# A four-layer vision kernel: spectral pieces that ride beside the scans, and the order inside a scan step

## The chip, the cores and the metric

One core of one Trainium2 chip runs the whole kernel. The metric is the device time of one execution in microseconds (us). The kernel before takes 27,082.73 us (median of three runs, 27,078.75 to 27,084.66). All arithmetic is in fp32.

## The reference, cut to what matters

Eight images of 64 x 64 pixels with 96 channels go through four residual layers, each on a group-normalised input:

```python
x = x + L0(gn(x))   # selective scan: 192 channels x 16 states, four scan directions
x = x + L1(gn(x))   # chunked scan
x = x + L2(gn(x))   # selective scan again, other weights
x = x + L3(gn(x))   # spectral: upsample x2, W1, quadratic, W2, low pass, every second pixel

def step(h, inp):                     # inside L0 and L2
    dA = exp(dt[..., None] * A)
    h = h * dA + (dt * u)[..., None] * b
    y = einsum('bkdn,bkn->bkd', h, c)
```

The four directions k = 0 to 3 are: along the rows, along the columns, along the rows backwards, along the columns backwards. For k = 1 and 3 the reference transposes the image ("wh"), so position 0, 1, 2, ... of the scan are pixels 64 floats apart in the kernel's row-major tiles.

In L3 the Fourier transforms are fixed 64 x 128 and 128 x 64 matrices, so that the layer is a chain of matmuls: up along one axis, up along the other, a hidden layer of 384 with a square, a mix back to 96, down along one axis, down along the other, and the residual.

## The kernel before, in words

The eight images are worked one after the other. For each one the program runs L0, L1 and L2 and the work between them. L3 of an image is not run there: it is cut into small pieces which are slipped into the two selective scans of the *next* image. So the two scans of image 0 have no pieces, the other 14 have; the L3 of the last image runs alone at the end (`spectral_layer`).

**A selective scan** (`selective_scan`) has 32 steps: four directions k times eight chunks c of 512 positions. A step has six units n = 0 to 5. One unit holds 32 channels x 16 states, as 128 partitions x 4 groups of 512 positions. The global unit is t = 6 i + n in step i. The order is written out by hand (`manual_schedule`); every engine works its own queue strictly in that order. Per unit:

- ACT: `decays(t, p)` (L855), two exps for each of two PSUM tiles `da0` and `da1`; `leave` (L886) copies the last column of h to `state`; `enter` (L826) puts the start state of a later unit in place.
- DVE: `scan(t, p)` (L870), two scans of 1026; `with_b` (L840) makes `db` = du x b, on DVE for four units of six and on POOL for n = 2 and 5.
- POOL: `h = h * c` (L891), after `state` has been copied out of h. Five `h` buffers.
- PE: `spread(t)` (L834) copies du to all partitions in PSUM (`pu`, tag "misc").

Per step, `total_y(i, hf)` sums over the states on PE (L898 adds the earlier y, L908 twelve matmuls) into `py`; the sum for units 0 to 2 is issued in unit 3, that for units 3 to 5 in unit 0 of the next step. ACT copies `py` to `y`: at L993 in unit 4, and at L1007 in unit 1. Both are `nc.scalar.copy(*sums)`. Before the change the one in unit 4 stands **ahead** of the exps of that unit, the one in unit 1 behind the first pair of them.

`prepare(i)` is a generator that makes a step's inputs two steps ahead, one part at each `prepare_part` call: matmul `pv` (L742), copy to `raw` (L747), matmul `pv` (L751), copy (L755), then the transfers `bcd` and `b`, two softplus (L775) with the change of activation table before and after them, `dd`, the transfers `dx` and `c`, `du` on POOL (L793 for wh steps, L799 for row steps), `dud`, `du2`, and the second `dx`.

PSUM has eight banks: `da0` and `da1` take three each, `py` one, `misc` one. The `py` bank is shared, in this order, by `total_y`, the `pv` of `prepare`, and most of the pieces; each waits until the one before it has been copied out by ACT.

**The pieces** (`slow_layer`, run by `Beside`). A piece is some matmuls into one PSUM bank (`begin`) and one ACT operation that empties it (`end`); some have a transfer as load before them or as store behind. First scan of an image: 16 x (T, A) (`rows`: transpose, up), two empty places, then 15 columns groups `cols`; second scan: 17 `cols`, two empty places, 16 x E (`ends`). One `cols` before is seven pieces: D, h, h, h, m, m, L (down_h; three hidden; two halves of the mix, each 8 matmuls and a copy of 192; lower). So the two scans have 139 and 137 pieces, and a step takes four or five. The places of a step are:

1. begin in unit 1 after the first exps, end at the end of unit 1 (bank py)
2. begin at the start of unit 2, end in the middle of it (py)
3. begin in the middle of unit 2, end at its end (py)
4. begin at the start of unit 4, end in the middle of it (misc)
5. begin at the start of unit 5, end right after (misc), only in steps with five pieces

All transfers of the pieces are issued by SP (`nc.sync.dma_start`): L451, L484, L495, L569, L581, L583, L614. Loads are issued up to four pieces ahead (`ends`: one), stores when the next piece begins (`flush`).

For wh steps, `view` reads u or y with the position running along the column, that is 64 floats apart, and `cut` gives the 512 positions of a chunk as 8 columns x 64 rows.

Of the kernel before, what the change touches and what calls it, by code (L numbers as in the profile page):

```python
# [17 lines left out]
DM = 96  # L18
# [4 lines left out]
LC = 512  # L23
# [44 lines left out]
def tile_vision_stack(  # L68
# [19 lines left out]
    nc = tc.nc  # L88
# [337 lines left out]

    def cut(t, wh):

        return t.rearrange("p (w h) -> p w h", h=64) if wh else t
# [3 lines left out]
    def slow_layer(prev):  # L433
# [12 lines left out]
        def rows(j):  # L446

            def load():
                if j % 2 == 0:
                    live["xs", j] = xs = wide("sx")[:DM]  # L450
                    nc.sync.dma_start(xs, xd[:, j * 256 : j * 256 + 512])  # L451
# [31 lines left out]
            def store():  # L483
                nc.sync.dma_start(  # L484
# [6 lines left out]
        def cols(n):  # L491

            def load():
                live["c1"] = c1 = narrow("sc", "x1")[:64]
                nc.sync.dma_start(c1, x1d[:, 4 * n : 4 * n + 4])  # L495
# [30 lines left out]
            for p in range(2):  # L526

                def mix(ps, p=p):
                    for i in range(2):
                        at = (2 * p + i) * 128  # L530
                        po = ps[:, i * DM : i * DM + DM]
                        nc.tensor.matmul(
                            po, live["x2"][:, at : at + 128], w12, start=True, stop=False
                        )
                        for m in range(3):
                            nc.tensor.matmul(
                                po,
                                live["f"][m][:, at : at + 128],
                                w2q[:, m, :],
                                start=False,  # L540
                                stop=(m == 2),
                            )

                def mixed(ps, p=p):
                    if p == 0:
                        live["g"] = narrow("sg", "g")
                    nc.scalar.copy(
                        live["g"][:, 2 * p : 2 * p + 2, :].rearrange("p i c -> p (i c)"),
                        ps[:, : 2 * DM],
                    )  # L550

                ops.append((None, None, mix, mixed, None, 0))
# [15 lines left out]
            def store():  # L568
                nc.sync.dma_start(  # L569
# [6 lines left out]
        def ends(j):  # L576

            def load():
                if j % 2 == 0:
                    live["xr", j // 2] = xr = wide("sr")[:DM]  # L580
                    nc.sync.dma_start(xr, xd[:, j * 256 : j * 256 + 512])  # L581
                live["g2", j] = g2 = narrow("s3", "g" if j % 2 else "x1")
                nc.sync.dma_start(g2, g2d[:, 4 * j : 4 * j + 4])  # L583
# [29 lines left out]
            def store():  # L613
                nc.sync.dma_start(  # L614
# [14 lines left out]
    class Beside:  # L629

        def __init__(self, ops):
            self.ops, self.at, self.waiting, self.loaded = ops, 0, None, 0
# [22 lines left out]
        def flush(self):  # L655
            if self.waiting:
                self.waiting()
                self.waiting = None

        def begin(self, pool, tag):  # L660
# [3 lines left out]
            if op:  # L664
                ps = pool.tile([128, LC], F32, name="ps", tag=tag)
                op[2](ps)
                self.flush()
                self.open = (op, ps)
            else:
                self.flush()  # L670
                self.open = (None, None)

        def end(self):
# [4 lines left out]
            if op:  # L678
                op[3](ps)
                self.waiting = op[4]  # L680
            self.at += 1
            if self.loaded <= self.at < len(self.ops):
                self.flush()
                while self.loaded <= self.at:
                    self.load(self.loaded)
# [4 lines left out]
    def selective_scan(w, wdt, a, d, u, y, beside):  # L690
# [23 lines left out]
        with (  # L714
# [14 lines left out]
            def prepare(i):  # L729
# [3 lines left out]
                uv = [view(u[:, hf, :], wh, at, LC) for hf in range(2)]  # L733
# [13 lines left out]
                nc.scalar.copy(raw[:DM, 1, :], pv[:DM])  # L747
# [7 lines left out]
                nc.scalar.copy(raw[:, 0, :], pv)  # L755
# [137 lines left out]
            def total_y(i, hf):  # L893
# [7 lines left out]
                    view((u if k == 0 else y)[:, hf, :], wh, c * LC, LC),  # L901
# [4 lines left out]
                for g in range(NSG):  # L906
                    for q in range(3):
                        nc.tensor.matmul(  # L908
                            py[32 * q : 32 * q + 32, :],
                            red,  # L910
                            hs[q][:, g, :],
# [3 lines left out]
                return view(y[:, hf, :], wh, c * LC, LC), cut(py, wh)  # L915
# [17 lines left out]
            with tc.tile_pool(name="p_conv", bufs=2, space=PSUM) as pvp:  # L933
# [13 lines left out]
                for _ in range(5):  # L947
# [6 lines left out]
                for _ in range(2):  # L954
# [8 lines left out]
            with tc.tile_pool(name="p_da", bufs=1, space=PSUM) as pap:  # L963
# [12 lines left out]
                for t in range(total + 2):  # L976
# [5 lines left out]
                    elif n == 5 and quota > 4:  # L982
# [789 lines left out]
```

## Time and profile before

| | us |
|---|---|
| median of the runs | 27,082.73 |
| the profiled execution's own time | 27,082.74 |
| its span | 27,080.9 |
| 16 selective scans, first to last DVE scan, together | 19,215 |
| one scan without pieces (image 0) | 1,195.2 and 1,194.9 |
| scans with pieces, first of an image | 1,197 to 1,204 |
| scans with pieces, second of an image | 1,203 to 1,207 |
| a step: first DVE scan to the first of the next, without pieces, from the fifth on | 37.57 mean |
| the shortest steps | 36.25 |

A step's length is read from the timeline of DVE: twelve scans (L870) make a step, and the start of the first one is its beginning. The table's scans are the stretches from the first of 384 scans to the end of the last. The lines of the timeline merge instructions that follow each other; the bracket at the end is the idle time before them and what ended it.

### The profile page before, as it was taken

The numbers are of one execution on the slowest core, as the hardware profiler recorded it, in microseconds if no ns is written. First come the engines' busy times: TensorE is split into PE (matmuls) and PEld (weight loads), VectorE is DVE, ScalarE is ACT, GpSimd is POOL, SyncE is SP. The second block draws the span as 40 slices with busy tenths as digits, with TensorE's granted clock in tenths as the row PEclk, the third lists the DMA queues.
The fourth block names the chain that finished last, engine by engine and source line by source line (L and its number), as shares of the span: only waits on it lengthen the run. The fifth ranks groups of instructions, "written<-read, shape, count | busy, mean of one in ns | idle before, by whom it ended". The sixth has DMA issues, their size and how long they took to land. (4 is left out here: it accounts for less than half of the span.)

```text
span 27080.9 us, 283056 instructions
## 1 busy us (share of the span) xinstructions
PE 22624.0 (84%) x91061; PEld 8150.5 (30%) x91061; DVE 23966.2 (88%) x17105; ACT 16539.7 (61%) x29953; POOL 21781.7 (80%) x8360
## 2 busy tenths in 40 slices
PE   7787788888888888888888888888888888888888
PEld 2141122422224222242222422224222342223424
DVE  8989899798997989979898898988989889898896
ACT  5656566466665656556565565655656556565564
POOL 8949898498984979859797697976979769797694
PEclk7687777877778777787777877778777787778878
DMA  4415454154541545415453254532545325453252
GB/s 121 119 30 124 114 130 117 31 131 122 132 111 35 133 117 137 103 44 132 116 136 98 50 132 118 135 92 56 133 119 134 85 62 133 118 134 78 70 133 67
DMA packets 1681704, 2831.72 MB, mean 105 GB/s; under 512 B 434984, under 2 KB 478280, under 8 KB 1675616
## 3 DMA queue, kind: packets, MB, share of 16 engines
q1 hardware_dynamic: 1663584, 2807.32, 41.9%
q8 instruction: 730, 11.96, 0.2%
q10 hardware_dynamic: 16640, 6.29, 0.1%
q14 instruction: 750, 6.14, 0.1%
HBM read 2385.11 MB, written 427.49 MB: 104 GB/s over the span
## 5 line engine op out<-in xcount | busy, mean ns | idle before, releaser
L870 DVE TENSOR_TENSOR_SCAN h<-da,db 128x1026 f32<-128x1026 f32 x6144 | 13765.8, 2282 | 900.6 <-ACT da L855 479.2
L891 POOL TENSOR_TENSOR h<-h,c 128x2048 f32<-128x2048 f32 x3072 | 12769.4, 4174 | 726.0 <-ACT state L886 510.1
L908 PE MATMUL py<-h,cst 128*32 128x512 f32 x24576 | 5301.4, 795 | 69.9 <-POOL h L891 69.8
L855 ACT ACTIVATE da<-dx,a2s 128x512 f32<-128x512 f32 x6144 | 4236.4, 690 | 1508.7 <-DVE h L870 1366.6
L855 ACT ACTIVATE da<-dx,a0s 128x512 f32<-128x512 f32 x6144 | 4235.8, 690 | 1481.8 <-DVE h L870 1344.3
L840 POOL TENSOR_TENSOR db<-du,b 128x2048 f32<-128x2048 f32 x1024 | 4648.2, 4539 | 567.6 <-ACT db L826 567.6
L840 DVE TENSOR_TENSOR db<-pu,b 128x2048 f32<-128x2048 f32 x2048 | 4643.9, 2268 | 110.9 <-PE pu L834 100.6
L834 PE MATMUL pu<-du,cst 32*128 32x512 f32 x4096 | 3239.2, 881 | 1007.4 <-DVE db L840 799.9
L908 PEld LDWEIGHTS py<-h,cst 128*32 128x32 f32 x24576 | 1175.0, 142 | 4827.3 <-issue 4517.4
L751 PE MATMUL pv<-u,wk 96*128 96x512 f32 x2048 | 1816.9, 1030 | 688.4 <-ACT raw L747 685.8
L898 PE MATMUL py<-y,cst 96*96 96x512 f32 x1536 | 1517.0, 1084 | 397.9 <-ACT raw L755 395.4
L834 PEld LDWEIGHTS pu<-du,cst 32*128 32x128 f32 x4096 | 790.4, 239 | 3079.7 <-issue 1361.9
L742 PE MATMUL pv<-u,wk 96*96 96x512 f32 x2048 | 1452.4, 838 | 186.7 <-ACT y L993 142.6
L1285 ACT ACTIVATE sg<-sg 128x768 f32<-128x768 f32 x1024 | 819.6, 800 | 859.1 <-PE sg L1269 859.1
L993 ACT COPY y<-py 96x512 f32<-96x512 f32 x512 | 417.5, 815 | 1411.4 <-PE py L908 1411.4
L516 PE MATMUL ps<-s,w3as 96*128 96x512 f32 x1344 | 912.4, 767 | 327.7 <-ACT sf L523 188.1
L1239 POOL TENSOR_TENSOR ce<-ec,cr 112x512 f32<-112x512 f32 x256 | 530.8, 2074 | 719.1 <-ACT ec L1237 700.8
L1317 DVE TENSOR_TENSOR wt<-wt,cbm 128x768 f32<-128x768 f32 x1024 | 985.3, 997 | 136.6 <-ACT wt L1286 136.1
L886 ACT COPY state<-h 128x4 f32<-128x4 f32 x3072 | 597.5, 194 | 782.5 <-DVE h L870 776.8
L751 PEld LDWEIGHTS pv<-u,wk 96*128 96x128 f32 x2048 | 540.6, 291 | 1740.2 <-ACT raw L747 1212.5
L319 POOL TENSOR_SCALAR xn<-xs,sb 96x512 f32<-96x512 f32 x192 | 198.1, 1033 | 991.7 <-PE pz L324 495.6
L1216 POOL TENSOR_TENSOR rr<-lr,cc 128x768 f32<-128x768 f32 x256 | 376.6, 1471 | 754.1 <-ACT lr L1214 749.2
(241 smaller groups left out, 30790.9 us busy)
## 6 DMA issues: line engine op xcount, KB each, us to landing
dx<-dd SPq DMA_DIRECT2D x4096, 192.0 KB
b<-bcd SPq DMA_DIRECT2D x2048, 256.0 KB
c<-bcd SPq DMA_DIRECT2D x2048, 256.0 KB
du<-dud SPq DMA_DIRECT2D x2048, 128.0 KB
dd<-raw SPq DMA_DIRECT2D x1024, 192.0 KB
dud<-du SPq DMA_DIRECT2D x512, 128.0 KB
xd<-xs SPq DMA_DIRECT2D x256, 192.0 KB
cr<-bcd SPq DMA_DIRECT2D x1536, 32.0 KB
```

The costliest lines, as they stand in the source:

```text
L516: nc.tensor.matmul(ps, w3as[:, m * 128 : (m + 1) * 128], live["x2"], start=True, stop=True)
L742: nc.tensor.matmul(pv[:DM], weights[k][:, hi, 128:], uv[hi], start=(hi == 0), stop=(hi == 1))
L751: nc.tensor.matmul(pv, weights[k][:, hi, :128], uv[hi], start=(hi == 0), stop=(hi == 1))
L834: nc.tensor.matmul(pu, sel[rows, :], m["du"][rows, n // 3, :], start=True, stop=True)
L840: (nc.gpsimd if pool else nc.vector).tensor_mul(groups(m["db", n]), (m["du2"][:, n // 3, :] if pool else m["pu"]) .unsqueeze(1) .to_broadc ...
L855: nc.scalar.activation(dst[:, g, :LC], made[i]["dx"][n // 3][:, n % 3, :], AF.Exp, scale=av4[:, k, n, gs : gs + 1],)
L870: nc.vector.tensor_tensor_scan(made[i]["h", n][:, at][:, way], das[p][:, rev : 2 * SEG + rev][:, way], made[i]["db", n][:, at][:, way], 0. ...
L891: nc.gpsimd.tensor_mul(h, h, made[i]["c"])
L898: nc.tensor.matmul(py, skip[:, hf, :] if k == 0 else ident[:DM, :DM], view((u if k == 0 else y)[:, hf, :], wh, c * LC, LC), start=True, st ...
L908: nc.tensor.matmul(py[32 * q : 32 * q + 32, :], red, hs[q][:, g, :], start=False, stop=(g == NSG - 1),)
L1285: nc.scalar.activation(sg, sg, AF.Abs)
L1317: nc.vector.tensor_mul(it["wt"], it["wt"], m["cbm"][:, j : j + 1, :].to_broadcast([128, RK, Q]),)
```

## The change

Four things, three in the scan step and one in the pieces.

1. **Pieces.** All seven transfers are issued by ACT (`nc.scalar.dma_start`). The two halves m, m become one piece of 16 matmuls and one copy of 384. A store is issued right behind its copy; `flush` is gone. There is no fifth place: the scans now have 124 and 120 pieces, three or four in a step.
2. **y's copy in unit 4** (was L993) moves behind the first pair of exps of that unit.
3. **prepare in eight parts** in place of seven: the copy to `raw` at L747 is cut from the matmul at L751 by a new `yield`. Both copies to `raw` now stand at the end of a unit (4 and 5), behind all exps of it; the `pv` matmuls stand at the start of units 4 and 5. The second copy, `bcd` and `b` come in unit 5 rather than in unit 0 of the next step. The `spread` for unit 0 of the next step moves from the start of unit 5 to unit 4, ahead of the first `pv`.
4. **Columns.** For wh steps PE reads u and y with `near`: for each of the 64 rows, 8 neighbouring floats. The results in PSUM are then in the order (row, column). `turn_back` reads them in column order for the copies to `raw` (ACT reads PSUM 8 floats apart, writes one after the other), and the L908 matmuls of wh steps write PSUM 8 floats apart. y's copies of wh steps read PSUM straight and write runs of 8, where before they wrote single floats 64 apart.

```diff
+    def near(t, wh, at, n):
+        if not wh:
+            return t[:, at : at + n]
+        return t.rearrange("p (h w) -> p h w", w=64)[:, :, at // 64 : (at + n) // 64]
+    def turn_back(t, wh, n):
+        return t.rearrange("p (h w) -> p w h", w=n // 64) if wh else t
...
-                nc.sync.dma_start(c1, x1d[:, 4 * n : 4 * n + 4])
+                nc.scalar.dma_start(c1, x1d[:, 4 * n : 4 * n + 4])
...
-            for p in range(2):
-                def mix(ps, p=p):
-                    for i in range(2):
+            def mix(ps):
+                for i in range(4):
...
+            def mixed(ps):
+                live["g"] = narrow("sg", "g")
+                nc.scalar.copy(live["g"].rearrange("p i c -> p (i c)"), ps[:, : 4 * DM])
...
             if op:
                 op[3](ps)
-                self.waiting = op[4]
+                if op[4]:
+                    op[4]()
             self.at += 1
-            if self.loaded <= self.at < len(self.ops):
-                self.flush()
-                while self.loaded <= self.at:
-                    self.load(self.loaded)
+            while self.loaded <= self.at < len(self.ops):
+                self.load(self.loaded)
...
-                uv = [view(u[:, hf, :], wh, at, LC) for hf in range(2)]
+                uv = [near(u[:, hf, :], wh, at, LC) for hf in range(2)]
...
-                nc.scalar.copy(raw[:DM, 1, :], pv[:DM])
+                nc.scalar.copy(cut(raw[:DM, 1, :], wh), turn_back(pv[:DM], wh, LC))
+                yield
...
-                nc.scalar.copy(raw[:, 0, :], pv)
+                nc.scalar.copy(cut(raw[:, 0, :], wh), turn_back(pv, wh, LC))
...
-                    view((u if k == 0 else y)[:, hf, :], wh, c * LC, LC),
+                    near((u if k == 0 else y)[:, hf, :], wh, c * LC, LC),
...
-                            py[32 * q : 32 * q + 32, :],
+                            turn_back(py[32 * q : 32 * q + 32, :], wh, LC),
                             red,
-                            hs[q][:, g, :],
+                            cut(hs[q][:, g, :], wh),
...
-                return view(y[:, hf, :], wh, c * LC, LC), cut(py, wh)
+                py = py.rearrange("p (h w) -> p h w", h=64) if wh else py
+                return near(y[:, hf, :], wh, c * LC, LC), py
...
                     if n == 2 and quota > 1:
                         other.begin(pyp, "py")
-                    elif n == 5 and quota > 4:
-                        other.begin(pmp, "misc")
-                    if n in (0, 3, 5) and ahead:
+                    if n in (0, 3) and ahead:
                         spread(t + 1)
...
                     elif n == 4:
-                        nc.scalar.copy(*sums)
                         if quota > 3:
                             other.begin(pmp, "misc")
+                        if t + 2 < total:
+                            spread(t + 2)
                         prepare_part(i + 2)
-                    if n == 5:
-                        other.end()
+                    elif n == 5:
+                        prepare_part(i + 2)
                     if t < total:
                         scan(t, 0)
...
                     elif n == 4:
+                        nc.scalar.copy(*sums)
                         other.end()
-                    elif n == 0:
-                        prepare_part(i + 1)
-                    elif n == 5:
-                        prepare_part(i + 2)
...
                     if n in (1, 2):
                         other.end()
+                    if n in (4, 5):
+                        prepare_part(i + 2)
                     if n in (0, 1, 5):
                         prepare_part(i + 1)
```

The calls ahead of the loop follow: six parts of `prepare(0)` where there were five, and four parts of `prepare(1)` where there were two.

## The prediction

> **What bounds the kernel now.** I read the page first, for the busy shares, then the groups, then who waits for whom, and last the timeline of one step engine by engine. The page's first part:
>
> ```profile
> PE 22624.0 (84%) x91061; PEld 8150.5 (30%) x91061; DVE 23966.2 (88%) x17105; ACT 16539.7 (61%) x29953; POOL 21781.7 (80%) x8360
> ```
>
> No engine is full. The costliest groups say where the time lies:
>
> ```profile
> L870 DVE TENSOR_TENSOR_SCAN h<-da,db 128x1026 f32<-128x1026 f32 x6144 | 13765.8, 2282 | 900.6 <-ACT da L855 479.2
> L891 POOL TENSOR_TENSOR h<-h,c 128x2048 f32<-128x2048 f32 x3072 | 12769.4, 4174 | 726.0 <-ACT state L886 510.1
> L993 ACT COPY y<-py 96x512 f32<-96x512 f32 x512 | 417.5, 815 | 1411.4 <-PE py L908 1411.4
> ```
>
> The 16 selective scans take 19,215 of the span's 27,080.9 us, and all edits are in them; the other 7,866 us I leave as they are. Inside a scan DVE and POOL do nearly the same amount: in a plain step of 37.55 us (timeline below) POOL idles only 0.88. The question is who makes those two wait, and the table of waits names ACT and PE:
>
> ```profile
> ACT y L993 <- PE py L908: 1411.4, 477, 6.6
> PE py L898 <- ACT raw L755: 551.1, 479, 3.6
> POOL h L891 <- ACT state L886: 510.1, 429, 3.7
> DVE h L870 <- ACT da L855: 479.2, 563, 7.8
> ACT sg L547 <- PE ps L536: 404.6, 343, 3.3
> ACT sr L588 <- DMA sr<-xd: 168.8, 21, 11.1
> ```
>
> ACT stands at y's copy 477 times, 3 us each; the exps that the next DVE scan needs are queued behind it. One plain step (no pieces, a wh step) from the timelines of DVE, ACT and POOL:
>
> ```profile
> 604.77 4.48 DVE L870 TENSOR_TENSOR_SCAN h<-da,db 128x1026 f32<-128x1026 f32 x2 [0.81 <-ACT da L855]
> ...
> 623.27 4.71 DVE L870 TENSOR_TENSOR_SCAN h<-da,db 128x1026 f32<-128x1026 f32 x2 [0.49 <-PE py L908]
> ```
> ```profile
> 602.43 1.05 ACT L993 COPY y<-py 96x512 f32<-96x512 f32 x1 [3.59 <-PE py L908]
> 603.27 1.42 ACT L855 ACTIVATE da<-dx,a0s 128x512 f32<-128x512 f32 x2
> ...
> 615.22 0.58 ACT L755 COPY raw<-pv 128x512 f32<-128x512 f32 x1
> ...
> 617.67 1.28 ACT L775 ACT_TABLE_LOAD   x1
> ...
> 621.62 1.42 ACT L855 ACTIVATE da<-dx,a0s 128x512 f32<-128x512 f32 x2
> ```
> ```profile
> 624.36 8.28 POOL L891 TENSOR_TENSOR h<-h,c 128x2048 f32<-128x2048 f32 x2 [0.88 <-ACT state L886]
> ```
>
> Three stalls: scan of unit 5 waits 0.81 for exps that stood behind y's copy; scan of unit 2 waits 0.49 for `total_y` to free an h buffer, which began late because its bank was held until the raw copy at 615.22; and POOL waits 0.88 for the state copy of unit 1, late for the same reason.
>
> **Part 1, the step.** Y's copy behind the exps: scan of unit 4 ended at 601.7, so the exps start there and not at 603.27, and the 0.81 goes. What is late next is the copy itself, which ends about where it did (603.3 against 603.5), so that the matmul `pv` behind it is not held longer. The second raw copy leaves unit 0: it stands at the end of unit 5, some 5 us earlier, so `total_y` waits for POOL alone (its last product ended at 614.81) and may do L898 before that; L898 began at 615.85. It then ends by 620.2 + its 5.4, minus what L898 has done ahead: about 621 in place of 623.1. The 0.49 goes; what then ends last is the exps behind the table loads (621.62 + 1.41 = 623.03, scan of unit 1 ends at 622.8), 0.3 later than ideal, as in the shortest steps of the trace. State of unit 1 follows 0.4 sooner. So a plain step becomes what POOL needs: 37.55 - 0.88 = 36.67 in wh steps and 0.51 less where du is the row form (2.37 in place of 2.88), mean 36.4. DVE can follow: 36.25 occurs. The timetable for all that follows, zero where POOL begins du: du to 2.9, products h3 to h5 at 4.15 each to 15.3, db 4.5, h0 to h2 to 32.2, db to 36.7, without a gap. The sums of units 0 to 2 end 5.6 after the h2 before (-4.5), at 1.1; those of 3 to 5 end 5.5 after 15.3, at 20.8. Unit 2 begins there, for its h buffer; counted on with 6.77 and 4.43 us (units with and without a db on DVE) and back by 36.7, units 4, 5, 0, 1, 2, 3 begin at -2.3, 2.1, 8.9, 15.6, 20.8, 27.6. Where is the cover thin? Raw copies now wait for PE with exps queued behind: `total_y` ends 1.1, y's copy 1.9, du 2.9, spread to 4.0, `pv` L742 to 6.0, raw copy 6.6, `pv` L751 (3.78) to 10.4, raw copy 11.0; the exps behind it are due to end at scan start 15.6 and the softplus chain needs them begun by 11.9. A margin of 0.9 us, lost if L742 takes its strided 3.65. SP is moved too: `bcd` and the four `b` now go ahead of the second `dx`. `dx` lands at about 22, exps need it at 23.
>
> Per step over all scans: 512 x 36.4, less 2.9 for each scan's shorter last step, is 18,590; the scans now take 19,215. **Room: 625 us.** It is shared by all stalls of today, the fifth place and the loads that come late included.
>
> **Part 2, columns.** Strided reading by PE costs today: the same L742 for a row step and for a wh step,
>
> ```profile
> 302.43 1.96 PE L742 MATMUL pv<-u,wk 96*96 96x512 f32 x4 [0.75 <-ACT y L993]
> ```
> ```profile
> 978.25 3.65 PE L742 MATMUL pv<-u,wk 96*96 96x512 f32 x4 [0.75 <-ACT y L993]
> ```
>
> I take 1.96 for runs of 8, bounds 1.96 and 3.65. Y's copies of wh steps take 1.05 and write singles; with runs of 8, 0.58 to 1.05, I take 0.58. Raw copies now read PSUM 8 apart: 0.58 to 1.05, and I take 0.8 from the middle, as no row shows it. These are off the path while the margin above holds. Then L908 in wh steps writes PSUM 8 floats apart. No row shows such a write. Below, no cost: its 24 records take 5.1 to 5.7. Above, the ratio of the strided reads, 3.65 / 1.96 = 1.86: 9.5. A gain is excluded, since the reads of h stay straight. I take no cost: the strided row is a read from another memory, while the write differs from L908's own row in nothing but the order, and its stream is slow: the shortest record, 590 ns for 512 columns, is one float per partition each 1.15 ns. The other end is a rival below.
> Here a page of the Trainium skill speaks against this change ("PSUM — Partial Sum Buffer", Specifications): it gives PSUM lines of 8 bytes and says that "any non-contiguous AP slows matmuls significantly". It gives no figure; taken at the reads' ratio, the sum by it is the rival's, and by the rows it is mine.
>
> **Part 3, pieces on ACT.** Issuing costs time on the issuing engine:
>
> ```profile
> L1597 ACTq DMA_DIRECT2D tok<-in_x_dram x16: 427/531/606, 0.7 to 23425.1; - x16
> L569 SPq DMA_DIRECT2D g2d<-sg x224: 615/623/730, 3818.4 to 26524.3; - x112
> ```
>
> So 0.4 to 0.6 us each, and 64 transfers in a scan: two in a step, 1 us of ACT. ACT idles some 11 us of a step, so the sum is harmless; the place matters. In places 1 to 3 the exps behind are not due for 2 us or more. In place 4 they are: exps of unit 5's second half are due when scan half one ends, and y's copy, the piece's copy (0.5 to 0.7) and the exps (1.4) fill that time already. L's store and the second h's load fall there about 16 times per image: 16 x 0.8 x 7 = 90 us. In the built program each transfer signals one of eight semaphores in turn and waits until the one before it on the same semaphore has landed; in place 2 that one is the first `dx` of the step, issued by SP in unit 1 and landing about when ACT gets there. Bounds 0 and 2 us for each of some 49; I take 0.6: 30 us.
>
> The mix: half a mix takes PE 2.0 us (16 records; 3.5 where PE starts cold), the whole 4.1. Counting pieces off (124 and 120 over 32 steps), the 32 mixes of an image fall 8, 9, 8 and 7 times on places 1 to 4. From the same timetable: place 1, PE 21.5 to 25.6, exps end 27.5, due 27.6, the state copy that POOL wants at 28.1 slips when L with its store follows: 0.4. Place 2: PE 24 to 28.1, state copy 28.8: 0.7. Place 3: PE done before its bank is wanted: 0.2. Place 4: PE 1.1 to 5.2, exps end 7.5 where 4.3 was due: 3.2, of which POOL's lag hides some: 2.6. Sum 3.2 + 6.3 + 1.6 + 18.2 = 29 per image, 205 us over seven.
>
> The last steps (E pieces): `sr` is loaded one piece ahead, and its landing (median 5.6 us after issue) is longer than the 2.5 us between places 1 and 2; ACT waits as today (168.8 in the table), 2.6 us in each of three steps, and about 4 in the one where E begins, where today's step takes 47.8 to 52.7: 12 x 7 = 83 us. T and A: loads are four pieces ahead and no longer behind SP's waits; nothing.
>
> **Sum.** 27,080.9 - 625 + 90 + 30 + 205 + 83 = 26,864. The execution's own time is 1.8 above its span, and equals the median of the runs (27,082.7): I predict **26,870 us**, 0.8% faster.
>
> **Rivals.** *A, strided PSUM writes are slow (slower).* PE is busy 1,019 of 1,207 us in a scan with pieces, 31.8 in a step. Two sums at 9.5 in place of 5.1 add 8.8 in wh steps, L742 gives 1.7 back: 38.9, the longest engine, and with its in-order waits about 40. Against my 37.2 for such a step that is 2.8 x 224, and 1 x 32 in the plain ones: 660, so 27,520. It decides from a group of about 8.4 us. For it: PE reads pay 1.86; against it: the slow stream. *B, ACT's order eats the room:* ACT is the engine all three others wait for in the table, and this change gives it transfers, a longer mix wait and raw copies that wait for PE. If the 408 us of losses are 1.5 times that, almost nothing is left (27,070); at twice, 27,270. For it: L547's waits, 343 of 448 copies already; against it: those halves at places 1 and 2 cost nothing in today's steps (36.3 to 36.7 us). *C, the losses hide:* steps after a late one run at 36.25 today, so POOL's lag may swallow all but place 4's half: losses 130, 26,590.
>
> **How the numbers follow.** Mine 0.40 (own range 26,700 to 27,020), C 0.18, A 0.20, B 0.22, of which 0.08 within 0.2% (54 us, about what a measurement tells from no change) and 0.14 above. Faster 0.58, same 0.08, slower 0.34. The range 26,600 to 27,500 leaves out the end of C and the far part of A.
>
> **What would show it.** Right: the wait of y's copy for PE falls well under 1,411; raw copy no longer ends PE's idle time before L898; plain steps 36.3 to 36.7; L742 at 1.96 in wh steps; waits of the mix copy grow to some 3 us each. Wrong: L908's group above 8 us in wh steps; plain steps above 37; waits of ACT for transfers in places 1 to 4; DVE waiting for exps more than the 479 us of today.

## The result, and the profile after

The changed kernel takes **28,279 us** (median of four runs, 28,264 to 28,313) against 27,083 us: a ratio of 1.0444, 95% interval 1.0426 to 1.0462. Forecast were 26,870 us in a range of 26,600 to 27,500. It is 4.4% slower, and outside the range.

The same views as before, now of the changed kernel (its line numbers: scans L867, products L888, exps L852, y's copies L1012 in unit 4 and L1004 in unit 1, dx L779, b and c L761, sums L905). The page's first part and costliest groups:

```profile
PE 22101.8 (78%) x91061; PEld 8508.7 (30%) x91061; DVE 23983.3 (85%) x17105; ACT 16349.2 (58%) x29729; POOL 21764.8 (77%) x8360
...
L867 DVE TENSOR_TENSOR_SCAN h<-da,db 128x1026 f32<-128x1026 f32 x6144 | 13781.4, 2283 | 2024.9 <-ACT da L852 1639.7
L888 POOL TENSOR_TENSOR h<-h,c 128x2048 f32<-128x2048 f32 x3072 | 12747.2, 4170 | 1971.6 <-issue 1687.0
```

DVE and POOL do as much as before, but the idle time ahead of the scans has grown from 900.6 to 2,024.9 us. The groups of y's copy in unit 4, and of the matmuls that add the earlier y; ahead of the latter's row stands that of before, L898:

```profile
L1012 ACT COPY y<-py 96x512 f32<-96x512 f32 x512 | 296.4, 579 | 271.7 <-PE py L905 269.4
```
```profile
L898 PE MATMUL py<-y,cst 96*96 96x512 f32 x1536 | 1517.0, 1084 | 397.9 <-ACT raw L755 395.4
...
L895 PE MATMUL py<-y,cst 96*96 96x512 f32 x1536 | 1327.8, 961 | 7.4 <-ACT y L1012 2.9 <-ACT raw L752 2.6
```

The two waits that the step was to lose are gone: 1,411.4 us of ACT have become 269.4, and the 395.4 us of PE behind the raw copy are 2.6. The table of waits shows what came instead:

```profile
POOL h L888 <- issue: 1687.0, 309, 12.7
DVE h L867 <- ACT da L852: 1639.7, 917, 9.9
...
ACT da L852 <- DMA dx<-dd: 1184.0, 233, 11.1
...
ACT sg L554 <- PE ps L544: 909.8, 209, 5.9
```

DVE waits for exps (479.2 before), exps wait for the transfers of dx (no such line among the 200 largest before), and the mix's copy waits longer (404.6 before). Read by scans, from DVE's timeline, the two scans without pieces fell from 1,195 to 1,160 us, and the 14 with pieces rose: the first scans of an image from 1,199 to 1,301 in the mean, the second ones from 1,204 to 1,287. The time outside the scans hardly moved. So the step itself became what was forecast, and the pieces cost more than they were given. Who holds dx back is in the queue waits of SP:

```profile
SPq L779 <- DMA sc<-x1d: 750.9, 56, 16.8
...
SPq L779 <- DMA x1d<-sw: 552.6, 49, 11.7
SPq L779 <- DMA g2d<-sg: 511.9, 49, 11.6
...
SPq L761 <- DMA sc<-x1d: 440.6, 63, 7.8
```

SP, about to issue dx (L779) or b and c (L761), waits for transfers of the pieces (`sc`, `x1d`, `g2d`), which ACT issues and whose data dx has nothing to do with. One such place, from the timelines of SP, ACT and DVE:

```profile
9098.33 11.48 SPq L779 DMA_DIRECT2D dx<-dd  x4
9109.91 0.36 SPq L782 DMA_DIRECT2D dd<-raw  x1
```
```profile
9106.20 0.47 ACT L568 COPY sg<-ps 64x384 f32<-64x384 f32 x1
9106.70 0.62 ACTq L573 DMA_DIRECT2D g2d<-sg  x1
9112.79 1.42 ACT L852 ACTIVATE da<-dx,a2s 128x512 f32<-128x512 f32 x2 [6.12 <-DMA dx<-dd]
```
```profile
9114.24 4.48 DVE L867 TENSOR_TENSOR_SCAN h<-da,db 128x1026 f32<-128x1026 f32 x2 [3.43 <-ACT da L852]
```

The four transfers of dx, 1.8 us of issuing elsewhere, take 11.48: two go out at once, the third only at 9,109, when the store that ACT issued at 9,106.7 has landed. ACT then stands 6.12 us at the exps, DVE 3.43 at the scan. Both kinds of transfer signal the same eight semaphores in turn, and each waits for the one eight before it: the trace's records name eight semaphores for the program's 15,905 transfers, 1,988 or 1,989 on each, and the store and the third dx have the same one, which was complete at 9,109.01, 0.02 us before that dx went out. The store has its turn ahead of that dx, though ACT comes to it 8 us after SP was ready. The other way round there was nothing: ACT waited 2 us in all ahead of its 912 issues.

### The profile page after: what moved, and what is told of

Same layout as the page of the kernel before. It is cut to its first block, busy times and chain, and to the rows that moved or that the text cites. A ratio compares the mean times of both kernels' runs of the same rounds, so it can differ in the third digit from the quotient of the medians.

```text
span 28262.6 us, 282461 instructions
## 1 busy us (share of the span) xinstructions
PE 22101.8 (78%) x91061; PEld 8508.7 (30%) x91061; DVE 23983.3 (85%) x17105; ACT 16349.2 (58%) x29729; POOL 21764.8 (77%) x8360
## 5 line engine op out<-in xcount | busy, mean ns | idle before, releaser
L867 DVE TENSOR_TENSOR_SCAN h<-da,db 128x1026 f32<-128x1026 f32 x6144 | 13781.4, 2283 | 2024.9 <-ACT da L852 1639.7
L888 POOL TENSOR_TENSOR h<-h,c 128x2048 f32<-128x2048 f32 x3072 | 12747.2, 4170 | 1971.6 <-issue 1687.0
L905 PE MATMUL py<-h,cst 128*32 128x512 f32 x24576 | 5437.5, 764 | 620.3 <-POOL h L888 619.7
L852 ACT ACTIVATE da<-dx,a0s 128x512 f32<-128x512 f32 x6144 | 4237.7, 690 | 2194.1 <-DVE h L867 1328.0
L852 ACT ACTIVATE da<-dx,a2s 128x512 f32<-128x512 f32 x6144 | 4237.2, 690 | 1916.3 <-DVE h L867 1283.0
L831 PE MATMUL pu<-du,cst 32*128 32x512 f32 x4096 | 2938.0, 804 | 1534.9 <-DVE db L837 1084.3
L905 PEld LDWEIGHTS py<-h,cst 128*32 128x32 f32 x24576 | 1253.6, 136 | 5206.0 <-issue 3614.9
L831 PEld LDWEIGHTS pu<-du,cst 32*128 32x128 f32 x4096 | 734.6, 223 | 3280.6 <-DVE db L837 1690.7
L526 PE MATMUL ps<-s,w3as 96*128 96x512 f32 x1344 | 1064.5, 884 | 802.7 <-ACT s L519 335.6
L748 PE MATMUL pv<-u,wk 96*128 96x512 f32 x2048 | 1259.3, 746 | 393.0 <-ACT raw L743 393.0
L895 PE MATMUL py<-y,cst 96*96 96x512 f32 x1536 | 1327.8, 961 | 7.4 <-ACT y L1012 2.9
L738 PE MATMUL pv<-u,wk 96*96 96x512 f32 x2048 | 1154.7, 692 | 66.3 <-ACT y L1012 24.3
L544 PE MATMUL ps<-w3bs,sf 128*128 128x96 f32 x5376 | 1090.4, 361 | 0.0
L544 PEld LDWEIGHTS ps<-w3bs,sf 128*128 128x128 f32 x5376 | 1012.1, 274 | 0.0
```

What stands on the lines that cost most here:

```text
L526: nc.tensor.matmul(ps, w3as[:, m * 128 : (m + 1) * 128], live["x2"], start=True, stop=True)
L544: nc.tensor.matmul(po, live["f"][m][:, at : at + 128], w2q[:, m, :], start=False, stop=(m == 2),)
L738: nc.tensor.matmul(pv[:DM], weights[k][:, hi, 128:], uv[hi], start=(hi == 0), stop=(hi == 1))
L748: nc.tensor.matmul(pv, weights[k][:, hi, :128], uv[hi], start=(hi == 0), stop=(hi == 1))
L831: nc.tensor.matmul(pu, sel[rows, :], m["du"][rows, n // 3, :], start=True, stop=True)
L852: nc.scalar.activation(dst[:, g, :LC], made[i]["dx"][n // 3][:, n % 3, :], AF.Exp, scale=av4[:, k, n, gs : gs + 1],)
```

## The experiments

Each runs beside the kernel before on the same chip; ratios are to that kernel, with their 95% intervals. It took 27,081 to 27,090 us beside them (medians); where us are given against it, they are against the 27,083 of the first comparison. Three theories: **S**, SP's step transfers stand behind ACT's through the shared semaphores; **M**, the mix in one piece; **O**, the order on SP's queue, b ahead of the second dx. **A** is the time that ACT spends on issuing.

### The transfers of the pieces

*All seven by SP again, the rest as changed.*

```diff
-                nc.scalar.dma_start(c1, x1d[:, 4 * n : 4 * n + 4])
+                nc.sync.dma_start(c1, x1d[:, 4 * n : 4 * n + 4])
```

> The changed kernel, with the seven transfers of the pieces issued by SP again; the step, the columns and the mix in one piece stay as changed. Theory S (SP's step transfers stand behind ACT's transfers, because both kinds signal the same eight semaphores in turn and a transfer waits for the one eight before it): the scans with pieces fall from 1,278-1,306 us to 1,165-1,200, the waits of the exps for dx (1,184 us) go, and the time is 26,750 us (26,600 to 26,950). Theory M (the mix in one piece is what costs): the time stays above 27,700. Theory O (b ahead of the second dx on SP's queue is what costs): above 27,700 as well, with the waits for dx still there.

Measured: 27,267 us, ratio 1.0067 (1.0052 to 1.0082). The issuing engine is worth 1,012 us, but theory S promised some 500 us more. The waits of exps for dx fell from 1,184 to 169 us:

```profile
L852 ACT ACTIVATE da<-dx,a0s 128x512 f32<-128x512 f32 x6144 | 4239.0, 690 | 1573.1 <-DVE h L867 1404.3 <-DMA dx<-dd 64.8 <-issue 0.3
L852 ACT ACTIVATE da<-dx,a2s 128x512 f32<-128x512 f32 x6144 | 4238.8, 690 | 1448.2 <-DVE h L867 1239.2 <-DMA dx<-dd 103.8 <-issue 0.8
```

Scans with pieces still take 1,211 and 1,225 (first and second scans, means), plain ones 1,159: something else costs them some 60 us each.

*The transfers by ACT alone, on the kernel before.*

```diff
-                nc.sync.dma_start(c1, x1d[:, 4 * n : 4 * n + 4])
+                nc.scalar.dma_start(c1, x1d[:, 4 * n : 4 * n + 4])
```

> The kernel before, with the seven transfers of the pieces issued by ACT and nothing else changed (mix in halves, fifth place, old step). Theory S: slower by about the same 1,000 us or more as in the changed kernel, 27,900 to 28,300, with SP waiting for transfers of the pieces ahead of dx and c. Theory M and theory O: within 150 us of the kernel before, 27,080 to 27,230, as neither the mix nor the order on SP has changed.

Measured: 27,349 us, 1.0096 (1.0081 to 1.0111). Slower, as S says, but by 266 us, not by 1,000. The same edit costs nearly four times as much in the changed step.

*ACT's time without the transfers.*

```diff
+        def idle():
+            scr = pool[0].tile([DM, 96], F32, name="scr", tag="scr", bufs=1)
+            for _ in range(2):
+                nc.scalar.copy(scr, cst[:DM, :96])
...
                 nc.sync.dma_start(c1, x1d[:, 4 * n : 4 * n + 4])
+                idle()
```

> As the run with the pieces' transfers on SP, and at each place where a transfer is issued ACT also makes two small copies (96 x 96) into a scratch tile, about as long as the issue of a transfer (0.4 to 0.6 us) and with no transfer. What is computed stays the same. Theory A (the time that ACT spends on issuing, at its place ahead of exps, is what costs): the time is near the changed kernel's, above 27,900. Theory S: at most 100 us above the run without the copies, so 26,750 to 26,950.

Measured: 27,324 us, 1.0091 (1.0076 to 1.0106), 58 us above the run without the copies. Two copies take ACT 0.54 us, one issue 0.49 (median in the changed kernel). Theory A falls.

*A transfer that nobody needs.*

```diff
+        def mark():
+            scr = pool[0].tile([1, 128], F32, name="scr", tag="scr", bufs=1)
+            nc.scalar.dma_start(scr, cst[:1, :128])
...
                 nc.sync.dma_start(c1, x1d[:, 4 * n : 4 * n + 4])
+                mark()
```

> As the run with the pieces' transfers on SP, and at each place where a transfer is issued ACT issues one tiny transfer as well (512 bytes into a scratch tile that nobody reads). What is computed stays the same; no engine needs the data of these transfers. Theory S: they take their turn on the eight semaphores, SP's step transfers wait for them, and the time is near the changed kernel's: 27,800 to 28,300. Theory A: the same as the run with the two small copies, above 27,900 if A holds at all. If both are wrong (the bytes or the data dependence of the pieces' transfers matter): near 26,800.

Measured: 28,148 us, 1.0388 (1.0371 to 1.0406): 882 us more than without the marks. SP's queue waits in this run (dx is L790 here, b and c L772, dud L810):

```profile
SPq L790 <- DMA scr<-cst: 1622.7, 147, 16.0
...
SPq L772 <- DMA scr<-cst: 672.1, 105, 12.6
...
SPq L810 <- DMA scr<-cst: 365.0, 63, 8.1
```

`scr` is read by no instruction. SP waits for it for one reason only, that both are transfers with a turn on the same semaphores. That shows that S happens; the 882 us are not all its price, since in this run ACT waits for earlier marks too, where its next one stands in its queue:

```profile
ACT state L894 <- DMA scr<-cst: 105.4, 32, 8.2
ACT da L863 <- DMA scr<-cst: 71.3, 33, 4.5
```

The price of S in the changed kernel is read from the exchange of the issuing engine, above and in the next run.

*Dx ahead of bcd and b on SP, transfers by ACT; then the same with the transfers by SP.*

```diff
-                    if n in (4, 5):
-                        prepare_part(i + 2)
                     if n in (0, 1, 5):
                         prepare_part(i + 1)
+                    if n in (4, 5):
+                        prepare_part(i + 2)
```

> The changed kernel (transfers by ACT, one mix) with one thing exchanged at the end of unit 5: the second dx of the next step is issued by SP ahead of bcd and b, not behind them. Theory S alone (what SP waits for is ACT's transfers on the shared semaphores, wherever dx stands): 28,100 to 28,350. Theory S with O (the waits hurt because dx stands behind five more transfers that wait for a copy at the end of unit 5, so its lead is used up): 27,500 to 27,950.

> The changed kernel with the pieces' transfers by SP (27,267 us) and the second dx ahead of bcd and b on SP. With transfers by ACT that exchange gave 628 us. Theory S with O: without ACT's transfers dx has lead enough in most steps, only the waits of the exps for dx go (169 us in the run with the transfers by SP): 27,080 to 27,250. If O is a cost of its own: below 26,900.

Measured: 27,651 us with ACT's transfers, 1.0214 (1.0199 to 1.0229), 628 less than the changed kernel; 27,245 with SP's, 1.0059 (1.0045 to 1.0072), 22 less than without the exchange, too little to tell from nothing. So O alone is nothing that can be measured, and S with O is most of the loss: ACT's transfers cost 406 us where dx goes first and 1,012 where it stands behind five transfers more. With dx first the exps still wait for it:

```profile
ACT da L852 <- DMA dx<-dd: 687.3, 147, 7.9
```

*Loads by ACT, stores by SP.*

```diff
-                nc.scalar.dma_start(
+                nc.sync.dma_start(
                     g2d[4 * n : 4 * n + 4].rearrange("w h c -> h w c"), live["g"][:64]
                 )
```

> The changed kernel with the pieces' loads issued by ACT (448 transfers) and their stores by SP (448). Theory S, stores: a store waits on ACT's queue for its place in the unit, so SP's transfers behind it on the same semaphore wait longest for stores; with the stores on SP most of the 1,012 us goes: 27,300 to 27,650. If each transfer on ACT costs the same, whatever it waits for: half of it, 27,750 to 27,900. If the loads are what matters: above 28,000.

Measured: 27,718 us, 1.0238 (1.0220 to 1.0255). The stores' 448 transfers are worth 561 us, the loads' 448 the other 451. My guess that stores are the worse by far was wrong: the loads cost nearly as much. They too stand in ACT's order, which may be why; no run shows it.

### The mix

*One mix, on the kernel before.*

```diff
-            for p in range(2):
-                def mix(ps, p=p):
-                    for i in range(2):
+            def mix(ps):
+                for i in range(4):
...
-                    elif n == 5 and quota > 4:
-                        other.begin(pmp, "misc")
-                    if n == 5:
-                        other.end()
```

> The kernel before with the mix as one piece of 16 matmuls and one copy, and without the fifth place; transfers by SP, the step and the columns as before. Theory M (a mix in one piece often runs on a slow TensorE clock, 7.1 us instead of 3.8, and then costs its step about 4.3 us, of which the old step's slack of 1.3 us hides a part): about 110 such mixes at 3.1 and 49 at place 4 at 1.25 make 400, the fifth place gives back 100 to 150: 27,340 us (27,200 to 27,450). If the mix in one piece costs only the 205 us that the prediction gave it, the old step's slack hides nearly all of it: 26,930 to 27,090.

Measured: 27,160 us, 1.0028 (1.0017 to 1.0039). Between the two forecasts. Of its 224 mixes 38 ran on the slow clock, not the 110 that I had carried over from the changed step, where it is 109 of 224 (transfers by SP).

*A quarter of the mix, in the changed step.*

```diff
             def mix(ps):
-                for i in range(4):
+                for i in range(1):
...
-                nc.scalar.copy(live["g"].rearrange("p i c -> p (i c)"), ps[:, : 4 * DM])
+                nc.scalar.copy(live["g"], ps[:, None, :DM].to_broadcast([128, 4, DM]))
```

> The changed kernel with the pieces' transfers by SP, and of the mix only the first 4 of its 16 matmuls: their columns are copied to all four places, so the copy stays one of 384 and the number of pieces stays; the spectral layer's values are not the reference's. Theory M (the length of the mix on PE is what costs, 7.1 us on the slow clock, 3.8 on the full one): the mix takes 1.0 to 1.8 us and its steps lose nearly all of their 640 us of excess: 26,700 us (26,620 to 26,850). Rival: what costs is ACT's order in those steps (copy, squares, transfers), not the matmuls: 27,100 or more.

Measured: 26,664 us, 0.9844 (0.9831 to 0.9857), 603 us less than with the whole mix. This kernel leaves out three quarters of the mix. The number of pieces, their copies and transfers are the same: the length of the mix on PE is the cost. Steps are read here by what they contain; the table gives the time above 36.25 us, summed over the 14 scans with pieces (31 steps of each, the last one has no next), from DVE's scan starts:

| step contains | steps | changed kernel | transfers by SP | and a quarter mix |
|---|---|---|---|---|
| T, A | 63 | 295 | 7 | 10 |
| mix at place 1 | 56 | 471 | 201 | 17 |
| mix at place 2 | 63 | 260 | 112 | 16 |
| mix at place 3 | 49 | 238 | 203 | 15 |
| mix at place 4 | 49 | 138 | 125 | 13 |
| other columns pieces | 126 | 241 | 41 | 39 |
| E | 28 | 222 | 123 | 133 |
| sum | 434 | 1,865 | 811 | 243 |

Why a step with a mix takes 2.95 us above 36.25 (641 us in 217 steps, transfers by SP) and not the 0.9 forecast (205 in 224): in part PE's clock. Two mixes in the run with transfers by SP, from PE's timeline, one at place 1 and one at place 2:

```profile
7185.26 2.08 PE L526 MATMUL ps<-s,w3as 96*128 96x512 f32 x2 [2.57 <-ACT y L1004]
7188.12 2.08 PE L526 MATMUL ps<-s,w3as 96*128 96x512 f32 x2 [0.78 <-ACT sf L533]
7190.97 0.74 PE L540 MATMUL ps<-w,s 96*128 96x96 f32 x2 [0.78 <-ACT sf L533]
7191.51 1.49 PE L544 MATMUL ps<-w3bs,sf 128*128 128x96 f32 x6
...
7497.56 1.13 PE L526 MATMUL ps<-s,w3as 96*128 96x512 f32 x2
7499.46 0.46 PE L540 MATMUL ps<-w,s 96*128 96x96 f32 x2 [0.78 <-ACT sf L533]
7499.76 0.83 PE L544 MATMUL ps<-w3bs,sf 128*128 128x96 f32 x6
```

The same six matmuls take 1.49 us in the first and 0.83 in the second. Stretches of the same run, with the granted clock behind the five engines' busy times:

```profile
7191.00:7198.10 7.10, 7.10 (x33) 6.93 (x33) 4.93 (x3) 1.38 (x4) 6.97 (x2) 0.50 0.77 159
7496.00:7504.00 8.00, 6.66 (x43) 4.40 (x38) 7.56 (x5) 5.44 (x13) 6.08 (x2) 1.00 0.75 195
```

0.50 against 1.00. Ahead of the first, PE had stood idle for 2.57, 0.78 and 0.78 us. Where its clock fell and came back:

```profile
7180.70:7184.10 3.40, 1.99 (x7) 0.33 (x3) 3.40 (x2) 3.34 (x5) 3.40 (x2) 1.00 1.03 222
7184.10:7187.50 3.40, 2.08 (x2) 0.50 (x2) 3.06 (x3) 2.70 (x7) 3.40 (x2) 0.50 0.68 187
...
7201.20:7204.60 3.40, 3.40 (x14) 0.62 (x15) 3.30 (x2) 0.27 (x1) 3.40 (x2) 0.50 0.17 39
7204.60:7208.00 3.40, 3.09 (x20) 0.64 (x14) 3.40 (x3) 2.23 (x4) 2.59 (x1) 1.00 0.53 154
```

It fell at 7,184.1, 1.4 us after the last matmul, and was back only at 7,204.6, though PE had worked without a gap since 7,191.0. The Trainium skill says that the clock is halved after an idle window of about 3.4 us and comes back after as long a busy one ("TensorE: Matmul & The Clock Gate", Part 1). The trace agrees in the two levels, and the changes of the granted clock in this run lie 3.41 us apart or a multiple of that. It differs in what precedes a fall: of the 897 falls from the first selective scan to the last only 81 come after 3.41 us in which PE worked under 2% of the time; in half of them it had worked over 42% of it. Ahead of at least nine in ten of the rises it had worked all of it. A whole mix takes 3.8 us on the full clock and 7.1 on the half one (medians). What follows it, first on ACT and then on DVE:

```profile
7198.15 0.48 ACT L554 COPY sg<-ps 128x384 f32<-128x384 f32 x1 [5.74 <-PE ps L544]
```
```profile
7200.15 2.29 DVE L837 TENSOR_TENSOR db<-pu,b 128x2048 f32<-128x2048 f32 x1 [4.12 <-PE pu L831]
```

The exps of the next half unit are queued behind that copy, and the spread for unit 3 (L831) is queued on PE behind the mix: DVE stands 4.12 us. By place and clock (steps of the run with transfers by SP, mean length; the forecast is the cost above a plain step):

| place | mixes | on the slow clock | step, full clock | step, slow clock | forecast cost |
|---|---|---|---|---|---|
| 1 | 56 | 44 | 36.48 | 40.76 | 0.4 |
| 2 | 63 | 14 | 37.44 | 40.08 | 0.7 |
| 3 | 49 | 45 | 37.08 | 40.68 | 0.2 |
| 4 | 49 | 0 | 38.80 | none | 2.6 |

On the full clock the forecast costs are near (0.2, 1.2, 0.8 and 2.6 above 36.25). The slow clock adds 4.28 x 44 + 2.64 x 14 + 3.60 x 45 = 387 us; the other 254 of the 641 are what the mixes cost on the full clock, in place of the 205 forecast. At place 3 only four mixes ran on the full clock. The run of one mix in the old step gives the same picture: at place 2 its steps take 36.82 on the full and 40.15 on the slow clock (46 and 17 steps), at place 3 36.37 and 41.37 (35 and 14). No run kept PE busy ahead of a mix, so the clock's share rests on these comparisons within runs.

*The halves again (the code of the mix as before the change), transfers by SP, with a fifth place in unit 0; then y's copy back ahead of the exps as well.*

```diff
-                    elif n == 1 and t + 2 < total:
-                        spread(t + 2)
...
                     if n == 1:
+                        other.end()
+                        if t + 2 < total:
+                            spread(t + 2)
                         if t > 1:
                             nc.scalar.copy(*sums)
...
+                    if n == 0 and quota > 4:
+                        other.begin(pmp, "misc")
```
```diff
                     elif n == 4:
+                        nc.scalar.copy(*sums)
                         if quota > 3:
...
                     elif n == 4:
-                        nc.scalar.copy(*sums)
                         other.end()
```

> The changed kernel with the pieces' transfers by SP (27,267 us) and the mix in two halves again; the fifth place, for steps with five pieces, begins at the end of unit 0 and ends in unit 1 behind the first exps, in the bank of spread, and the spread for unit 3 stands behind it. Theory M: the steps with a mix lose their 640 us of excess, the halves and the fifth place cost 100 to 200: 26,780 us (26,650 to 26,900), faster than both. If the mix is not the cost: 27,200 or more.

> The run with the halves (changed kernel, transfers by SP, mix in halves, fifth place; 27,181 us) with y's copy of unit 4 back ahead of the exps, as in the kernel before. If y's copy behind the exps is what makes steps with pieces longer (the bank py and so the matmul pv are held longer, place 4 comes later): 26,900 to 27,080, plain scans back near 1,190. If it is prepare's eight parts or the new fifth place: 27,180 or more, by up to the 1.15 us that the copy gives a plain step.

Measured: 27,181 us, 1.0040 (1.0025 to 1.0055), and 27,316 us, 1.0080 (1.0065 to 1.0095). The halves with their new fifth place give back 86 us, not 490; each step of five pieces takes 37.0 to 41.3 us (means over the images). And y's copy is not what makes that version slow: without its move it is slower by 135. Plain scans took 1,163 us in the second run.

### The columns, and y's copy alone

*On the kernel before: all of the columns (the lines of the change's part 4); only prepare's half of them, without the last two lines shown; the columns and y's copy of unit 4 behind the exps.*

```diff
-                uv = [view(u[:, hf, :], wh, at, LC) for hf in range(2)]
+                uv = [near(u[:, hf, :], wh, at, LC) for hf in range(2)]
...
-                nc.scalar.copy(raw[:, 0, :], pv)
+                nc.scalar.copy(cut(raw[:, 0, :], wh), turn_back(pv, wh, LC))
...
-                            py[32 * q : 32 * q + 32, :],
+                            turn_back(py[32 * q : 32 * q + 32, :], wh, LC),
```

> The kernel before with the columns alone (part 4 of the change): PE reads u and y in runs of 8, writes the sums 8 floats apart, ACT turns them back. Expected by the prediction's step: columns are off the path, and at most the plain column steps (37.64 us) come down to the row steps (37.26): 256 x 0.38 = 97 us, so 26,985 to 27,085. If strided writes of PSUM cost anything on the path: above 27,100.

> The kernel before with prepare's half of the columns alone: PE reads u in runs of 8 for pv, ACT turns it back at the raw copies; the sums and y's copies as before. Theory P (PE's matmul pv, 4.2 us strided and 2.4 in runs for its four records, holds bank py and delays spread, sums and pieces behind it in PE's queue): most of the 220 us, 26,870 to 26,950. Theory Y (y's copies, 1.05 us and 0.58, and L898's reads): 27,000 to 27,090.

> As the run with the columns alone, and y's copy in unit 4 behind the first pair of exps (part 2), nothing else: prepare and the pieces as before. If POOL sets the plain step (the prediction's reading), the 0.81 us that DVE no longer waits is not seen, since POOL still loses its 0.88 to the raw copy in unit 0: within 100 us of the run with the columns alone. If y's copy is the stall that counts (1,411 us of ACT's waits): 512 x 0.8 = 410 us faster, about 26,600.

Measured: the columns alone **26,865 us, 0.9917 (0.9904 to 0.9931)**, faster than both kernels; prepare's half 27,000, 0.9967 (0.9954 to 0.9979); columns with y's copy 27,014, 0.9970 (0.9960 to 0.9981). My expectations were off for the first and the third; prepare's half came out at the lower edge of theory Y. The columns gave 218 us, not at most 97, with 83 from prepare and 135 from the sums and y's copies. Plain scans did not gain (1,194); scans with pieces fell to 1,183 and 1,189. The likely reason is that steps with pieces wait for PE and ACT, which the columns relieve. The groups of the run with the columns alone:

```profile
L752 PE MATMUL pv<-u,wk 96*96 96x512 f32 x2048 | 1014.2, 619 | 133.0 <-ACT y L1004 90.9 <-DMA wk<-wdt 21.0 <-ACT u L296 18.4
```
```profile
L1004 ACT COPY y<-py 96x512 f32<-96x512 f32 x512 | 297.4, 581 | 1353.5 <-PE py L918 1353.5
```

`pv` takes 619 ns a record (838 before), y's copy 581 ns (815 before), and ACT still stands 1,353.5 us at it. Sorted by the clock granted at the time, a `pv` record of a column scan (L742 before) took 1,035 ns on the full clock and 1,037 on the half one, of a row scan 592 and 1,061 (medians): reading 64 floats apart costs only where PE has its full clock. So L751, most of whose records run on the half clock in the old step, gained little (1,030 to 1,003 ns in the mean). With y's copy moved behind the exps, plain scans fall to 1,163, yet scans with pieces rise to 1,196 and 1,209: PE now waits more for the later copy ahead of its next matmul,

```profile
PE pv L752 <- ACT y L1025: 735.3, 388, 4.8
```

The stall that a plain step shows was worth its time in plain steps only.

## Why the prediction was wrong

**The step: right.** It forecast 36.4 us for a plain step in place of 37.55; plain scans went from 1,195 to 1,160 us, most of their steps to 36.25. The waits named as gone are gone. One part of the reasoning is simpler than it had it: beside the columns, y's copy without prepare's new parts (1,163) or those parts without y's copy (1,163) bring nearly all of it, both together 1,160. The raw copy does wait for `pv` now, as it feared (836.5 us of ACT at L743, 69.3 before); plain steps hide that, and what it costs in steps with pieces no run tells apart.

**Strided writes to PSUM: right, no cost.** The group of 24 matmuls takes 5.5 and 5.7 us (median, k = 1 and 3) against 5.7 and 5.4 in row scans. Sorted by the clock granted at the time, one record takes 592 ns on the full clock and 1,061 on the half one (medians), in column scans and in row scans alike. The raw copies take 581 and 578 ns in all four directions, so the 0.8 taken for them was too much. Rival A falls: it had the right sign, for a cost that is not there. Where the Trainium skill says that any non-contiguous access slows matmuls significantly ("PSUM — Partial Sum Buffer", Specifications), the measurement differs for fp32 written 8 floats apart.

**Pieces on ACT: wrong, the largest error.** The prediction gave 90 us for place 4 and 30 for the shared semaphores. The failing step is its sentence on place 2, that the transfer eight before is dx "issued by SP in unit 1 and landing about when ACT gets there": it costed ACT waiting for SP and not SP waiting for ACT. In the changed kernel the first direction cost nothing (2 us of ACT's waits). The second is the dear one: SP works ahead of ACT in the program's order, 8 us in the place shown, and everything behind the waiting transfer on SP's queue waits too. Against these 120 us the exchange of the issuing engine measured 1,012, some 58 of them ACT's own time by the run with the small copies. The prediction had all that was needed: the eight semaphores, five transfers now ahead of the second dx, "dx lands at about 22, exps need it at 23". A cover of 1 us against a wait of up to 16.8 us should have been priced. T and A, priced at "nothing", were 288 us of it.

**The mix: right mechanism, wrong size.** 205 us forecast, 603 measured. The costs by place hold on the full clock, roughly (254 us in all). The term left out is that 103 of 217 mixes run on the half clock, though "3.5 where PE starts cold" stood in the prediction for a half; it was carried to the whole as 4.1, never as 7.1.

**Columns: wrong, "off the path".** Alone they are worth 218 us. The path was read from a plain step; steps with pieces gained nearly all of it. That PE and ACT are on their path is the likely reading.

**The E pieces:** 83 forecast, 123 measured with SP's transfers, 222 with ACT's.

**The sum.** The room of 625 us was real: with a quarter mix and SP's transfers the kernel takes 26,664, which is 419 below the kernel before; 625 less 243 of other losses would be 382. What was put against the room was 408 and measured 1,865. Rival B had the right sign and twice the losses at most, rival C the wrong sign. Of the signs named in advance, "DVE waiting for exps more than the 479 us of today" came true, with 1,640.

**What stays open.** Why mixes run on the slow clock three times as often in the changed step as in the old (109 and 38 of 224). The slow stretch has moved from prepare to the pieces: of the 2,048 records of `pv`'s second matmul (L751 before, L748 after) 1,826 ran on the half clock in the run of one mix on the old step and 830 in the changed step (transfers by SP), of the 1,344 of the hidden pieces 237 and 573. What in the new order moves it is not shown. And of the 316 us between the halves in the changed step and the columns alone, the runs exclude y's copy but do not part prepare's eight parts from the new fifth place.

## What to carry to other kernels

Where a program's queues share their completion semaphores, as this one's do, a transfer moved to another engine's queue still takes its turn on them: look at which transfers of the *other* queue come eight places behind it, and how much lead the data has that they carry. A plain step is not the steps with extra work in them: cost each kind of step by itself, at the clock that PE has at that place. And when a bundle fails, run its parts alone; here one of four parts was worth 0.8%, and the others hid it.

## What the hardware showed that was not expected

- A transfer of 512 bytes that nobody reads, issued 896 times by the second queue, costs 882 us, through the semaphores that this program's queues share and ACT's waits for its own marks. The Trainium skill says of spreading transfers over engines that it only saves sequencer issue time ("DMA: Bandwidth & Descriptors", Rules for kernel authors); here the move to ACT cost 1,012.
- The granted clock fell to 0.50 only 1.4 us after PE's last matmul and stayed there for 20.5 us, through 13.6 us of work without a gap; the same mix took 7.1 us in place of 3.8.
- PE reading SBUF 64 floats apart takes 1,035 ns for a record of 512 columns at either clock; in runs it takes 592 on the full clock and 1,061 on the half one.
- ACT reads PSUM 8 floats apart as fast as one after the other, 581 ns for 512 columns in column scans and in row scans, and PE writes it so at no cost either, at either clock.
